# Four graph-network layers on 16 graphs: the first graph's PSUM copies get a chain of their own, and both halves of x are asked for first

## The chip, the core and the metric

The kernel runs on one core of one Trainium2 chip. The metric is the device time of one launch in microseconds. Times inside the profile count from the start of the profiled execution's span. The engines are called by the profile's names: PE (TensorE, matmuls and transposes), DVE (VectorE), ACT (ScalarE), POOL (GpSimd, which here mostly issues gathers), SP (SyncE, which issues most DMAs).

## The reference

There are 16 graphs with 1024 nodes and 64 features each: x is [16, 1024, 64], adj is [16, 1024, 1024] with weights between 0.05 and 1 on about 0.8% of its places and on the diagonal; all is float32. Four layers follow each other, each on the layer norm of what is there so far, and each is added to it:

```python
h = max(layernorm(x), 0); x = x + (adj @ h) @ W.T                  # layer 0
h = max(layernorm(x), 0)                                           # layer 1
m = relu(relu(h @ W1 + b1) @ W2 + b2); msg = relu(adj @ m)
x = x + gru(msg, h)                    # sigmoid gates r and z, tanh n
h = max(layernorm(x), 0)                                           # layer 2
T2 = 2 * adj @ (adj @ h) - h
x = x + (K0*h + K1*(adj @ h) + K2*T2) @ weight + bias
h = max(layernorm(x), 0)                                           # layer 3
# neighbours of a node: adj > 0 off the diagonal; a node with m > 10 of them
# drops every ceil(m/2)-th (and is dropped from theirs)
agg = 0.25*quantile25 + 0.5*quantile50 + 0.25*quantile75           # over neighbours, per feature
x = x + relu((h + agg) @ W1 + b1) @ W2 + b2
```

## The kernel before, in words

**A planner orders the work.** The kernel is written as Python generators, called chains. Each yields one instruction at a time, or a wish for a buffer from a stock, or a condition that it waits for, or a new key. The class `Weave` takes the heads of all chains, works out when each could start by costs that are written into the code (`Line.cost`: a DMA costs 0.4 us to issue, and its data count as there 2.0 us + bytes/150e3 later), picks the engine whose head can start first, and of its heads the one with the smallest key. The order in which instructions are picked is the order in which the engine runs them: every engine works its list from first to last. `Weave.ready` finds when an instruction can start from what earlier ones read and wrote. It compares ranges from the first to the last element, so two interleaved halves of a tile count as one place. The hardware's own waits come from the real places; the planner's view only sets the order. Nearly all instructions of the profile carry line 325, the line of the helper that emits them, so they are told apart by their tiles.

**The chains.** `transposing` loads the adjacency of a graph in eight blocks of 128 columns (512 KB each, on SP) and transposes them: per block two halves, of four PE transposes into one PSUM bank each (stock "tp" with two banks), then an ACT copy of the bank into the tile AT (L952), after which the bank goes back to its stock. The first eight blocks of the run are asked for at once: two in the tiles "block", six in tiles "G". `layering` runs `layers` for two graphs in turn: x is loaded into X in two halves, to even and odd places of the tile (L995–996), normalized (for graph 0 in a form that runs on DVE but for one ACT square root, `sd`), and multiplied with the AT tiles (`into`, one pair of matmuls for each tile; the aggregate goes from its bank to "wide"). Layers 1 and 2 follow. `coding` and `listing` turn AT into lists of neighbours (`there`, `code`, `cand`, `more`, `own`); the list `own` of a graph is done when DVE has converted it to integers. `gathering` then issues 72 indirect DMAs on POOL for each graph (L665) that fetch the neighbours' rows from the table which the graph's layer 2 has stored (L671). `quantiling` sorts them on DVE, and the closing layers and the store of out follow. At the end come a few gathers and scatters for nodes with many neighbours. A general path for other inputs stands under a condition and isn't run.

**Around the change.** Before the chains begin, weights are loaded and prepared: among others the DVE instructions for `k02ident` (L572) and four copies at L587 out of PSUM banks that the transposes need afterwards. In SP's list the first half of x stands first, then two blocks and five of the G blocks, then the second half of x, then the sixth G block. In ACT's list the square root `sd` of graph 0 stands between the third and the fourth copy into AT. The planner counts the second half of x as waiting for the first, as both write to the same range by its reckoning.

Of the kernel before, what the change touches and what calls it, by code (L numbers as in the profile page):

```python
# [16 lines left out]
AF = mybir.ActivationFunctionType  # L17
# [5 lines left out]
P = 128  # L23
N = 1024
NT = N // P
# [116 lines left out]
def batcher(n):  # L142

    full = 1
    while full < n:
        full *= 2
    layers, p = [], 1
    while p < full:
        k = p
        while k >= 1:  # L150
            layer = [(i + j, i + j + k) for j in range(k % p, full - k, 2 * k) for i in range(k)
                     if (i + j) // (2 * p) == (i + j + k) // (2 * p) and i + j + k < n]
            if layer:
                layers.append(layer)
            k //= 2
        p *= 2
    return layers


def needed(layers, places):  # L160

    live, kept = set(places), []
    for layer in reversed(layers):
        k = [(a, b, a in live, b in live) for a, b in layer if a in live or b in live]
        for a, b, _, _ in k:
            live |= {a, b}
        kept.append(k)
    return kept[::-1]


def progressions(s):

    found, top = [], max(s) + 1
    for st in sorted(s):
        found.append((frozenset([st]), (st, 0, 1, 0, 1)))
        for d in range(1, top):
            run = [st]
            while run[-1] + d in s:
                run.append(run[-1] + d)
                found.append((frozenset(run), (st, 0, 1, d, len(run))))  # L180
                for e in range(d * (len(run) - 1) + 1, top):
                    both, k = list(run), 1
                    while all(x + k * e in s for x in run):
                        both += [x + k * e for x in run]
                        k += 1
                        found.append((frozenset(both), (st, e, k, d, len(run))))
    return found
# [164 lines left out]
class Weave:  # L352
# [19 lines left out]
    def add(self, gen, key):  # L372
        self.chains.append(dict(gen=gen, key=key, op=None, want=None, value=None))
# [82 lines left out]
    def run(self):  # L456
        while True:
            before = None
            while before != (before := [(id(c["want"]), id(c["op"])) for c in self.chains]):
                for chain in sorted(self.chains, key=lambda c: c["key"]):  # L460
                    if not self.advance(chain):
                        self.chains.remove(chain)
            heads = [c for c in self.chains if c["op"]]
            if not heads:
                break
            best = {}
            for c in heads:
                op = c["op"]
                c["start"] = max(self.free.get(op.line, 0.0), op.ready)
                best[op.line] = min(best.get(op.line, 1e9), c["start"])  # L470
            line = min(best, key=best.get)
            chain = min((c for c in heads if c["op"].line is line and c["start"] <= best[line] + SLACK),
                        key=lambda c: c["key"])
            op, start = chain["op"], chain["start"]
            chain["op"], chain["value"] = None, self.issue(op, start, (chain["gen"].__name__, chain["key"]))
        assert not self.chains, [c["want"] for c in self.chains]
# [15 lines left out]
class Fast:  # L492
# [431 lines left out]
    def transposing(self, adj):  # L924

        D, T, S = self.D, self.T, self.S
        blocks = {}


        early = self.early  # L930

        def load(i):
            b, j = divmod(i, NT)
            blocks[i] = block = early.pop(0).rearrange("p (t m) -> p t m", m=P) if 2 <= i < NT else (yield "block")
            yield D.dma_start(block, adj[b, :, j * P:(j + 1) * P].rearrange("(t p) m -> p t m", p=P))

        total = GRAPHS * NT
        yield -1.0
        for i in range(NT):
            yield from load(i)  # L940
        for i in range(total):
            b, j = divmod(i, NT)
            yield float(b) - 3
            if NT <= i + 1 < total:
                yield from load(i + 1)
            block = blocks.pop(i)
            at = yield "AT"
            for half in range(2):
                bank = yield "tp"
                for q in range(4):  # L950
                    yield T.transpose(bank[:, q * P:(q + 1) * P], block[:, 4 * half + q, :], self.ident)
                yield S.activation(at[:, 512 * half:512 * half + 512], bank, AF.Copy)  # L952
                self.weave.give("tp", bank)
            if not 2 <= i < NT:
                self.weave.give("block", block)
            self.turned[b].append(at)

    def norm(self, w, h, X, then=None, early=False, order=range(NT)):

# [28 lines left out]
    def layers(self, w, b, x):  # L988

        T, V, S, D, give = self.T, self.V, self.S, self.D, self.weave.give  # L990
        ident = self.ident
        cols = [slice(0, 512), slice(512, N)]
        yield lambda: self.turns == b
        X = yield "X"
        for half in range(2):  # L995
            yield D.dma_start(X[:, half::2, :], x[b, cols[half], :].rearrange("(q p) f -> p q f", p=P))
        turned = self.turned[b]
        by_tile = [2 * (j % 4) + j // 4 for j in range(NT)]

# [26 lines left out]
        bank = yield "fm"  # L1026
# [6 lines left out]
        bank = yield "fm"  # L1033
# [8 lines left out]
        bank = yield "fm"  # L1042
# [8 lines left out]
        bank = yield "fm"  # L1051
# [4 lines left out]
        bank = yield "fm"  # L1056
# [37 lines left out]
        for v in (new, z):  # L1094
            first, bank = bank if sides else None, (yield "fm")
# [16 lines left out]
        bank = yield "fm"  # L1112
# [4 lines left out]
        bank = yield "fm"  # L1117
# [34 lines left out]
        bank = yield "fm"  # L1152
# [7 lines left out]
        X = last  # L1160
# [291 lines left out]
    def run(self, x, adj, nodemask, out):  # L1452
        self.out = out
        self.listed, self.paid, self.gathered, self.last, self.turns = {}, {}, [], [], 0
        self.fetched = []
        self.masked, self.coded = [0] * GRAPHS, {}
        self.turned = [[] for _ in range(GRAPHS)]
        self.sizes = dict.fromkeys(("hits", "bad", "m1", "pos", "off", "coef"), 0)
        for t, n in CLASSES + MANY:
            places = max(int(np.ceil(tau * (n - 1))) for tau in TAUS) + 1  # L1460
            for name, size in (("hits", 2 * (n - 1) * t), ("bad", (n - 1) * t), ("m1", t), ("pos", 4 * t),
                               ("off", 4 * places * t), ("coef", places * t)):
                self.sizes[name] = max(self.sizes[name], size)
        add = self.weave.add
        add(self.listing(nodemask), 0.0)
        add(self.transposing(adj), 0.0)
        add(self.coding(), 0.0)
        for w in range(2):
            add(self.layering(w, x), 0.0)
        add(self.gathering(), 0.0)  # L1470
        add(self.fetching(), 0.0)
        add(self.quantiling(), 0.0)
        self.weave.run()
# [624 lines left out]
```

## Time and profile before

| what | value |
|---|---|
| time, median of three runs | 1920.10 us (1913.11, 1920.10, 1929.66) |
| profiled execution | 1915.65 us, its span 1913.6 us |
| mean granted PE clock | 0.836 |
| DVE busy | 1616.6 us, 84% |
| PE busy | 1418.7 us, 74% |
| POOL busy | 1357.5 us, 71% |
| ACT busy | 1015.5 us, 53% |
| first transposes on PE, first gather on POOL | at 13.03 us, at 125.83 us |

A line of the timeline gives start and duration in us, the engine, the line, the operation, the tile written and the tiles read, how many alike follow each other, and in brackets for how long the engine stood idle before it and what ended that. A line of the list of waits gives the engine, its tile and line, what it waited for, then the sum, the number of times and the longest, in us. A line of the chain of waits gives start and duration in us of a piece of the path that ended last.

### The profile page before, as it was taken

How to read it: one execution, taken by the hardware profiler on the slowest of the kernel's cores; microseconds unless marked ns; L12 is line 12 of the kernel's file. 1: busy time of each engine (PE TensorE's matmuls, PEld its weight loads, DVE VectorE, ACT ScalarE, POOL GpSimd, SP SyncE). 2: the span in 40 equal slices, each digit the busy share in tenths (PEclk: the TensorE clock that was granted, in tenths of full speed). 3: DMA queues.
4: the chain of work that ended last, by engine and by line, in shares of the span. 5: the costliest groups of instructions: out<-in, count | busy, mean ns of one | idle time of the engine just before them, and what ended most of it. 6: DMA issues, size and time to landing. Idle time of an engine off the chain costs nothing.

```text
span 1913.6 us, 24539 instructions
## 1 busy us (share of the span) xinstructions
PE 1418.7 (74%) x6740; PEld 742.3 (39%) x6740; DVE 1616.6 (84%) x4699; ACT 1015.5 (53%) x2905; POOL 1357.5 (71%) x1315
## 2 busy tenths in 40 slices
PE   6888688878887988888888888888787853442314
PEld 2343335343434453434444444444343422231313
DVE  2755998769899889898999999998999899898866
ACT  3656666575766566666666575666666431121000
POOL 2027777777777777777777777777777777777772
PEclk8989797989998889899989898989999786556555
DMA  5233525343535444434444443435252413121110
GB/s 140 77 78 81 95 70 95 80 79 74 112 86 74 90 72 103 72 93 82 94 73 102 68 106 64 100 68 96 67 108 46 56 24 44 36 40 39 26 27 12
DMA packets 260192, 141.10 MB, mean 74 GB/s; under 512 B 91370, under 2 KB 239328, under 8 KB 260048
## 3 DMA queue, kind: packets, MB, share of 16 engines
q1 hardware_dynamic: 216720, 94.40, 21.2%
q0 software_dynamic: 42064, 44.37, 15.0%
q8 instruction: 57, 0.93, 0.2%
q10 hardware_dynamic: 1264, 0.68, 0.1%
q14 instruction: 87, 0.71, 0.1%
HBM read 120.18 MB, written 19.17 MB: 73 GB/s over the span
## 4 chain that ended last, share of the span: by engine, by line
DVE 57%; PE 19%; ACT 8%; issue 6%; DMA 5%; POOL 4%; SPq 0%; DVEq 0%; POOLq 0%; ACTq 0%
DVE G L325 22%; PE bank L325 19%; DVE net L325 7%; DVE L L325 4%; DVE cand L325 4%; ACT sq L325 4%; DVE wide L325 4%; POOL G L665 4%; DMA G<-table,own 3%; DVE st L325 2%; DMA X<-in_x 2%; DVE AT L325 1%; ACT there L325 1%; ACT L325 1%; DVE off L325 1%
## 5 line engine op out<-in xcount | busy, mean ns | idle before, releaser
L665 POOL DMA_INDIRECT G<-table,own x1274 | 1327.5, 1042 | 516.9 <-issue 299.9
L325 PE MATMUL bank<-AT,nodes 128*64 128x512 f32 x2048 | 576.9, 638 | 38.5 <-ACT nodes L325 30.3
L325 PE MATMUL bank<-G,c 128*128 128x256 f32 (+2 forms) x646 | 183.0, 423 | 148.1 <-DVE G L325 148.1
L325 PEld LDWEIGHTS bank<-AT,nodes 128*64 128x64 f32 x2048 | 162.9, 144 | 290.3 <-issue 190.5
L325 PE MATMUL bank<-c,block 128*128 128x128 f32 x976 | 194.3, 307 | 56.4 <-ACT AT L325 45.9
L325 DVE TENSOR_TENSOR G<-G 128x256 f32<-128x256 f32 (+5 forms) x401 | 211.2, 546 | 7.7
L325 PEld LDWEIGHTS bank<-c,block 128*128 128x128 f32 x976 | 128.3, 154 | 207.4 <-issue 138.8
L325 PEld LDWEIGHTS bank<-G,c 128*128 128x128 f32 x646 | 123.9, 233 | 192.8 <-DVE G L325 125.5
L325 ACT ACTIVATE AT<-bank 128x512 f32<-128x512 f32 x256 | 150.3, 588 | 84.8 <-PE bank L325 84.1
L325 ACT ACTIVATE nodes<-X,off,ri 128x64 f32<-128x64 f32 x360 | 140.9, 430 | 67.2 <-DVE off L325 67.2
L325 ACT ACTIVATE G<-G,coef 128x64 f32<-128x64 f32 x384 | 97.8, 339 | 108.8 <-DVE coef L325 108.8
L325 ACT ACTIVATE sq<-X,st 128x64 f32<-128x64 f32 x360 | 125.0, 347 | 48.3 <-DVE st L325 27.3
L325 DVE TENSOR_TENSOR net<-G 128x512 f32<-128x512 f32 (+8 forms) x246 | 143.5, 601 | 4.3 <-PE bank L325 1.4
L325 DVE TENSOR_TENSOR G<-G,net 128x512 f32<-128x512 f32 (+4 forms) x235 | 136.0, 598 | 4.6
L325 PE MATMUL bank<-wide,blocks 128*128 128x512 f32 x224 | 124.4, 656 | 20.0 <-DVE wide L325 11.8
L325 ACT ACTIVATE there<-AT 128x1024 f16<-128x1024 f32 x128 | 133.4, 1050 | 0.4
L325 PE MATMUL bank<-there,c 128*64 128x512 f16 x256 | 76.7, 431 | 59.3 <-DVE there L325 55.5
L325 ACT ACTIVATE off<-off 128x144 f32<-128x144 f32 (+5 forms) x76 | 22.9, 301 | 152.4 <-DVE off L325 151.2
L325 DVE SCALAR_TENSOR_TENSOR G<-bad,G 128x512 f32<-128x512 f32 (+2 forms) x161 | 100.4, 684 | 0.0
L325 DVE MAX8 L<-cand 128x8 f16<-128x103 f16 x384 | 91.8, 263 | 8.7
L325 ACT ACTIVATE wide<-bank 128x512 f32<-128x512 f32 (+2 forms) x86 | 49.0, 570 | 89.7 <-PE bank L325 89.5
L325 PE MATMUL bank<-wide,yo 64*64 64x128 f32 x512 | 64.7, 383 | 34.8 <-DVE wide L325 33.2
(216 smaller groups left out, 2226.1 us busy)
## 6 DMA issues: line engine op xcount, KB each, us to landing
block<-in_adj SPq DMA_DIRECT2D x122, 512.0 KB
G<-table,own POOLq DMA_INDIRECT x1274
rows<-pay SPq DMA_DIRECT2D x16, 632.0 KB
table<-pay SPq DMA_DIRECT2D x16, 264.0 KB
X<-in_x SPq DMA_DIRECT2D x32, 128.0 KB
yo<-rows SPq DMA_DIRECT2D x16, 256.0 KB
out<-yo SPq DMA_DIRECT2D x16, 256.0 KB
G<-in_adj SPq DMA_DIRECT2D x6, 512.0 KB
```

The lines of the kernel that those rows point to most:

```text
L325: return Op(self, lambda: f(*args, **kwargs), writes, reads, cost, later)
L665: return self.nc.gpsimd.indirect_dma_start(out=out, out_offset=None, in_=table, in_offset=bass.IndirectOffsetOnAxis(ap=at, axis=0))
```

## The change

There are two edits. In `transposing`, the copies of graph 0's banks into AT are no longer yielded behind the transposes: half, tile and bank are noted in `self.raw`, and a new chain, `copying`, yields the copies, gives the banks back and hands the finished tiles over. The tiles of later graphs are copied as before, but are handed over only when all eight tiles of graph 0 have been. In `layers`, the second half of x is told to the planner as writing nothing. So the planner lets it be issued without waiting for the first, and doesn't count the time until its data are there; that is so for all 16 graphs. Real dependencies are kept.

```diff
@@ transposing @@
                 for q in range(4):
                     yield T.transpose(bank[:, q * P:(q + 1) * P], block[:, 4 * half + q, :], self.ident)
+                if b == 0:
+                    self.raw.append((half, at, bank))
+                    continue
                 yield S.activation(at[:, 512 * half:512 * half + 512], bank, AF.Copy)
                 self.weave.give("tp", bank)
             if not 2 <= i < NT:
                 self.weave.give("block", block)
-            self.turned[b].append(at)
+            if b:
+                yield lambda: len(self.turned[0]) == NT
+                self.turned[b].append(at)
+
+    def copying(self):
+        yield -3.0
+        for i in range(2 * NT):
+            yield lambda: len(self.raw) > i
+            half, at, bank = self.raw[i]
+            yield self.S.activation(at[:, 512 * half:512 * half + 512], bank, AF.Copy)
+            self.weave.give("tp", bank)
+            if half:
+                self.turned[0].append(at)
@@ layers @@
         for half in range(2):
-            yield D.dma_start(X[:, half::2, :], x[b, cols[half], :].rearrange("(q p) f -> p q f", p=P))
+            load = D.dma_start(X[:, half::2, :], x[b, cols[half], :].rearrange("(q p) f -> p q f", p=P))
+            if half:
+                load.writes = []
+            yield load
@@ run @@
-        self.fetched = []
+        self.fetched, self.raw = [], []
...
         add(self.transposing(adj), 0.0)
+        add(self.copying(), 0.0)
```

Comparing the lists of both kernels: POOL's is the same throughout. In SP's list both halves of x of graph 0 now stand first, ahead of the blocks. In ACT's list `sd` stands ahead of all sixteen copies, and one table load is gone. In PE's list sixteen transposes come first, then pairs of matmuls alternate with eight transposes, and ten matmuls stand together at the end, where before a pair followed each set of four transposes. In DVE's list the seven instructions of graph 0's normalization stand among the preparations, the last of them ahead of `k02ident` and L587, and the first sum over X of a later graph stands earlier in three places. All lists are the same again from about the fifth graph on.

## The prediction

> **What bounds the kernel now.** I read the page first, to see which engines are full; then the table of stretches and the timeline of the first 50 us, since the diff edits only the first graph's work there; then the chain of waits over the first 130 us, to learn whether that start is on the path; and last the list of waits, to learn whether a shift of the start can reach the end.
>
> The page:
>
> ```profile
> span 1913.6 us, 24539 instructions
> PE 1418.7 (74%) x6740; PEld 742.3 (39%) x6740; DVE 1616.6 (84%) x4699; ACT 1015.5 (53%) x2905; POOL 1357.5 (71%) x1315
> DVE 57%; PE 19%; ACT 8%; issue 6%; DMA 5%; POOL 4%; SPq 0%; DVEq 0%; POOLq 0%; ACTq 0%
> ```
>
> The vector engine is the fullest and holds 57% of the chain that ended last. The list of waits says what POOL, the engine of the gathers, waits for:
>
> ```profile
> POOL G L665 <- issue: 299.9, 984, 0.3
> POOL G L665 <- DVE own L325: 110.7, 1, 110.7
> POOL G L665 <- PE bank L325: 47.2, 116, 2.3
> DVE st L325 <- DMA X<-in_x: 28.0, 11, 6.3
> ```
>
> POOL is idle for 110.7 us once, until the first gather at 125.83, and never again for more than 2.3 us: from there gathers follow each other every 0.95 + 0.30 = 1.25 us up to about 1881. So a first gather that comes earlier can move everything behind it, as long as each graph's table is ready when POOL gets to it.
>
> The start, in the timeline:
>
> ```profile
> 12.30 2.39 SPq L325 DMA_DIRECT2D X<-in_x  x1
> 16.73 1.28 ACT L325 ACT_TABLE_LOAD   x1
> 19.71 0.69 DVE L325 TENSOR_REDUCE st<-X 128x8 f32<-128x512 f32 x1 [6.05 <-DMA X<-in_x]
> 23.59 0.30 ACT L325 ACTIVATE sd<-va,eps 128x8 f32<-128x8 f32 x1 [5.59 <-DVE va L325]
> 24.43 1.11 PE L325 MATMUL bank<-c,G 128*128 128x128 f32 x4 [7.02 <-ACT AT L325]
> 30.08 0.66 PE L325 MATMUL bank<-c,G 128*128 128x128 f32 x4
> 43.38 2.80 PE L325 MATMUL bank<-AT,nodes 128*64 128x512 f32 x12
> 47.63 0.57 ACT L325 ACTIVATE wide<-bank 128x512 f32<-128x512 f32 x1
> ```
>
> The second half of x is asked for at 12.30, behind blocks that fill SP's queue. Its sum starts at 19.71; the normalization reaches the scalar engine (sd) at 23.59. That engine's order puts sd between copies of transposed tiles, so they stand still too, both transpose banks stay full, and TensorE idles 7.02 us. The chain of waits confirms it: the path runs through this X, then through 19 us of TensorE.
>
> ```profile
> 12.30 7.32 DMA X<-in_x
> 24.43 19.03 PE bank L325 x64
> ```
>
> **The change, part by part.** Comparing the issue orders of both kernels, engine by engine, the same instructions are there, except one table load fewer on the scalar engine. POOL's order is the same throughout; VectorE's is the same for the last 3226 entries of its list of 4442, TensorE's for the last 3267 of 4785, SyncE's from its 74th of 225. The differences end in about graph 5, near 550 us. Nothing later waits for a fixed time, so the end moves by what is left of the shift there.
>
> (1) X first. SP issues both halves at about 0.75 and 1.25 (the first half is asked for at 0.75 now). Landing: no row shows the second half so early. The late one took 7.32 with a full queue, which gives 8.6 as the upper bound; the first weight that TensorE waited for, asked for at 1.24, was there at 6.17, which I take. VectorE's chain (0.69 + 0.15 + 0.67 + 0.67 + 0.67 + 0.20 + 0.69 = 3.74 us, from its rows) then stands ahead of the constant k02ident and the four copies of L587 (1.36), which free the PSUM that the transposes wait for. They began at 13.03; I take 14.0 (13.0 if X is there at 5, 16.0 if at 8.6).
>
> What is late: the eight blocks, by 128 KB at the 266 GB/s of the stretch 0–25 us = 0.5 us. The last is needed by TensorE near 28 and lands near 22. Cover gone, the cost is 0.5.
>
> The Trainium skill, "DMA: Bandwidth & Descriptors", speaks against small rows ahead of larger ones: by Specifications a transfer below 512 B doesn't reach line rate, and "Why small descriptors are slow (HBM only)" gives a 256 B descriptor 27% overhead. A row of X is 64 floats, 256 B; by the rule the 0.5 us would be an estimated 0.6, and hidden as well. No run here shows the two rates apart.
>
> (2) Copies apart. Sixteen copies of 0.60 us follow each other now without sd in between, and TensorE's order changes: the first sixteen transposes of a tile pair still take 3.57, one pair of aggregation matmuls 0.93; then five rounds of eight transposes and a pair (1.32 + 0.93) plus eight more transposes, 12.6; then ten matmuls at 0.43 plus 0.2 of tail, 4.5. That is 21.6 us, from 14.0 to 35.6. Before, it ended at 43.38 + 2.80 = 46.2. Gain 10.6; with the starts of 13.0 and 16.0, 11.6 and 8.6. Of the gain 7.0 is the stall; 0.9 is the two slow sets of transposes after it (1.11 and 1.12 against 0.66); the rest is closer packing. The table load saved (1.28) costs nothing now: it lies in the wait for sd.
>
> (3) To the first gather. The aggregate's copy moves from 47.63 to about 37. Behind it, the scalar engine works without gaps worth naming until 63.50 (code), VectorE is 88% busy from 75 to 100 and TensorE 86% there and 91% from 100 to 125; block loads for graph 1 are triggered by transposes that are early too. So the whole 10.6 should reach 125.83. The new wait on graph 0's tiles costs nothing: they are all copied before graph 1's first tile is.
>
> (4) Given back. The scheduler no longer counts the landing of the second half, so it believes that a later graph's X is ready sooner. On VectorE, which is in order, three of the sums over a new X now stand right behind the conversion of own, the running graph's neighbours; queued behind that sum are the rest of the previous layer's add and of the running list of neighbours. The rows of before at the three places, and what follows the first:
>
> ```profile
> 131.31 0.69 DVE L325 TENSOR_REDUCE st<-X 128x8 f32<-128x512 f32 x1 [6.31 <-DMA X<-in_x]
> 181.21 0.24 DVE L325 TENSOR_TENSOR hits<-G,own 128x80 f32<-128x80 f32 x1 [8.18 <-DMA G<-table,own]
> 308.09 0.20 DVE L325 CAST own<-own 128x80 int32<-128x80 f32 x1
> 314.00 0.68 DVE L325 TENSOR_REDUCE st<-X 128x8 f32<-128x512 f32 x1
> 409.81 0.69 DVE L325 TENSOR_REDUCE st<-X 128x8 f32<-128x512 f32 x1 [4.59 <-DMA X<-in_x]
> ```
>
> At 131 four instructions (some 2 us), and at most 3.5 us with the smaller ones around them, move behind a wait that stays as long; they go into the 8.18 us that VectorE waits at 181.21. At 314.00 there is no wait now; moved up behind the conversion at 308.09, the sum waits up to 314.0 − 308.3 = 5.7. That is 0 to 5.7; I take 0, because from 325 to 425 VectorE is idle for 31 us (busy 69.18 of 100) and POOL needs the next table only 16 us after it is ready (399.34 against 415.52). At 409.81 the conversion stands at 399.34 and the sum would be reached at 400.4, so its wait grows from 4.6 to 9.4, by 0 to 4.8; afterwards VectorE is over 90% busy and a loss stays. I take the middle, 2.4, since POOL's margin of 14 to 16 us there covers a part.
>
> **Sum:** −10.6 + 2.4 = −8.2 us on the profiled execution, 1915.65 (span 1913.6 and 2.05 around it): 1907.4. The runs' median, 1920.1, is 4.5 above this execution; the same shift on it gives 1911.9, rounded 1912. Bounds: −11.6 + 0 and −8.6 + 5.7 + 4.8, so −12 to +2, or 1908 to 1922.
>
> **The rivals.**
>
> *A, hidden.* A start that is early ends in a wait for another engine. For: from graph 7 on the table is ready only 0.7 to 2.6 us before POOL needs it (802.91 against 805.76), so both sides bind, and a lag on either eats the gain. Against: both sides start early here. Price: the whole 8; 1918 to 1922, that is, about 1920.
>
> *B, more than the start.* POOL's 47.2 us of waits for TensorE's banks shrink because graphs 1 to 4 interleave better. If a fifth goes, −10.6 − 9.4 = −20: 1900. Against: each of these waits is small and most lie where the orders are alike.
>
> *C, slower.* The three sums of step 4 hold up VectorE's queue and nothing takes it in: 3.5 + 5.7 + 4.8 = 14.0 us lost, against a start gain of 8.6 to 10.6. That is +3.4 to +5.4, 1924 to 1926. It decides from the point where the conversion of own in graph 5 (600.93) comes later than before. For: VectorE holds 57% of the chain. Against: the wait at 181 and the idle time from 325 to 425.
>
> *D, not what it says.* Later graphs' halves are issued back to back already (398–400), so only graph 0's request moves. But the wait of 7 us is graph 0's, so this takes nothing away.
>
> **How the numbers follow.** My forecast, a gain of 4 to 12: 0.58. A: 0.15. B: 0.13. C: 0.14. Some 1% (19 us) is about what a measurement of this kernel can tell from no change; its three runs lie within 1913.11 and 1929.66. Faster than 1901: a fifth of the forecast's cases, by such scatter, 60% of B's and few of A's: 0.21. Slower than 1939: a third of C, by scatter: 0.05. The rest is 0.74. The range takes in the bounds 1908 to 1922, B's 1900 and most of C; the likeliest case's own range is 1908 to 1916.
>
> **What would show it.** Right: the first st<-X near 6 to 9 us, no TensorE gap above 2 us between 14 and 36, the first gather between 113 and 118, then the first gather of graph 5 (610.14) 6 to 12 earlier. Step 4 is seen in the wait of st<-X: it sums to 28.0 now, 7.1 of it before 30 us; above 21 + 14 = 35 C is at work. The prediction is wrong if the first gather moves by less than 6, or if it moves by 10 and the last gather doesn't.

## The result, and the profile after

The changed kernel is slower: a median of 1930.77 us over 20 runs (1912.48 to 1947.51) against 1916.51 us (1902.32 to 1939.40) over 20 runs of the kernel before on the same chip. The ratio is 1.0078, with a 95% interval of 1.0050 to 1.0107: some 15 us lost. This ratio, like those below, leaves out runs that took over 1.5% more than the fastest of their kernel, so it can differ from the quotient of the medians beside it, most for `x_first_again` below, where 5 of 12 runs are left. Its profiled execution took 1943.40 us, 12.6 above its own median, while that of before stood within 1 us of its median; so of the difference of the two profiles, 28 us, nearly half is the scatter of single executions.

The page of the kernel after:

```profile
span 1941.6 us, 24545 instructions
PE 1455.9 (75%) x6740; PEld 771.1 (40%) x6740; DVE 1615.1 (83%) x4699; ACT 1016.9 (52%) x2904; POOL 1358.7 (70%) x1315
DVE 51%; PE 23%; ACT 8%; DMA 6%; issue 6%; POOL 5%; SPq 1%; DVEq 0%; POOLq 0%; ACTq 0%
```

DVE, POOL and ACT are busy for as long as before. PE is busy for 37 us more with the same 6740 matmuls, and its share of the chain that ended last rose from 19% to 23%. The mean granted clock of PE is 0.814, where it was 0.836. So the same matmuls took longer. The list of waits:

```profile
POOL G L665 <- issue: 298.4, 978, 0.6
POOL G L665 <- PE bank L325: 174.2, 124, 97.0
DVE st L325 <- DMA X<-in_x: 37.9, 12, 11.0
```

The one long wait of POOL, until its first gather, is 97.0 us now (it was 110.7). The profile puts it down to a PE bank instead of `own`, so it stands in the second line; without it that line is 77.2, against 47.2 before. The timeline of the start, and the first gather:

```profile
0.75 0.99 SPq L325 DMA_DIRECT2D X<-in_x  x2
4.96 0.69 DVE L325 TENSOR_REDUCE st<-X 128x8 f32<-128x512 f32 x1 [1.98 <-DMA X<-in_x]
7.88 1.28 ACT L325 ACT_TABLE_LOAD   x1 [7.88 <-DMA wide<-in_L_gnn_W_hh]
9.85 0.30 ACT L325 ACTIVATE sd<-va,eps 128x8 f32<-128x8 f32 x1 [0.69 <-DVE va L325]
13.53 3.62 PE L325 MATMUL bank<-c,block 128*128 128x128 f32 x16 [1.13 <-issue]
29.24 4.51 PE L325 MATMUL bank<-AT,nodes 128*64 128x512 f32 x20
111.82 1.01 POOL L665 DMA_INDIRECT G<-table,own  x1 [96.98 <-PE bank L325]
```

The start did what it was to do. X is there at 4.96, `sd` runs before the first copy, the aggregation ends at 29.24 + 4.51 = 33.75 instead of 46.2, and the first gather comes at 111.82 instead of 125.83: 14.0 us won. Then they are lost. A good clock for that are the sixteen stores of the table at L671, one for each graph, in the timeline of SP:

| issue of the table's store, us | before | after | difference |
|---|---|---|---|
| graph 0 | 120.4 | 106.7 | −13.7 |
| graph 3 | 397.7 | 383.4 | −14.3 |
| graph 5 | 595.3 | 593.3 | −2.1 |
| graph 9 | 992.3 | 996.0 | +3.7 |
| graph 12 | 1287.7 | 1306.9 | +19.2 |
| graph 15 | 1580.1 | 1608.1 | +28.0 |

From the last store to the end of the span both take 333.5 us. So 12 us went between graphs 3 and 5, where the orders of the two kernels still differ, and 30 between graphs 5 and 15, where all lists are the same. The three places that the prediction's step 4 named, in the timeline of the kernel after, with the two gaps of PE that go with the second and third:

```profile
115.69 0.69 DVE L325 TENSOR_REDUCE st<-X 128x8 f32<-128x512 f32 x1 [5.82 <-DMA X<-in_x]
167.59 0.24 DVE L325 TENSOR_TENSOR hits<-G,own 128x80 f32<-128x80 f32 x1 [4.42 <-DMA G<-table,own]
302.09 0.69 DVE L325 TENSOR_REDUCE st<-X 128x8 f32<-128x512 f32 x1 [2.84 <-DMA X<-in_x]
303.95 0.68 PE L325 MATMUL bank<-wide,yo 64*64 64x128 f32 x2 [10.29 <-DVE wide L325]
393.35 0.69 DVE L325 TENSOR_REDUCE st<-X 128x8 f32<-128x512 f32 x1 [5.13 <-DMA X<-in_x]
401.95 0.64 PE L325 MATMUL bank<-there,c 128*64 128x512 f16 x2 [7.62 <-DVE there L325]
```

The wait of 8.18 at 181.21 has become 4.42 at 167.59: it took in the first place, as argued. At 302.09 there is a new wait of 2.84; PE, which needs a `wide` that is queued behind it on DVE, stands still for 10.29 us there, and for 4.07 at this place in the kernel before. At 393.35 the wait grew only from 4.59 to 5.13, and PE's 7.62 us behind it stand against 10.08 before.

What a wait of DVE for X does to PE can be read where it stands alone. The timeline of the kernel after at graph 10, from SP's, DVE's and PE's lines:

```profile
1094.05 0.37 SPq L671 DMA_DIRECT2D table<-pay  x1
1094.50 0.54 SPq L671 DMA_DIRECT2D rows<-pay  x1
1095.10 2.73 SPq L325 DMA_DIRECT2D X<-in_x  x2
1107.64 0.69 DVE L325 TENSOR_REDUCE st<-X 128x8 f32<-128x512 f32 x1 [3.42 <-DMA X<-in_x]
1109.16 0.64 PE L325 MATMUL bank<-there,c 128*64 128x512 f16 x2 [4.80 <-DVE there L325]
1110.53 3.67 PE L325 MATMUL bank<-wide,yo 64*64 64x128 f32 x30 [0.73 <-DVE wide L325]
1131.21 7.98 PE L325 MATMUL bank<-AT,nodes 128*64 128x512 f32 x32
```

X is asked for right behind 264 KB of table and 632 KB of rows on the same queue and is there 12 us later. DVE waits 3.42 us for it, PE 4.80 for DVE. And from then on PE is slow. The table of stretches of the kernel after; the last two columns are DMA, the one before them is the granted clock:

```profile
1100.00:1110.00 10.00, 5.00 (x30) 3.73 (x29) 5.89 (x26) 8.09 (x30) 7.30 (x8) 0.96 0.95 119
1110.00:1120.00 10.00, 9.47 (x46) 6.42 (x47) 9.18 (x45) 5.21 (x13) 5.37 (x6) 0.50 0.28 74
1120.00:1130.00 10.00, 10.00 (x30) 6.14 (x30) 3.97 (x20) 4.54 (x11) 3.82 (x5) 0.50 0.45 93
1140.00:1150.00 10.00, 9.60 (x38) 4.27 (x37) 9.87 (x26) 6.50 (x11) 7.56 (x9) 1.00 0.30 76
```

and the same instructions in the kernel before, one graph earlier, where PE had waited 0.82 us for `there`:

```profile
1010.00:1020.00 10.00, 9.92 (x53) 6.00 (x55) 9.07 (x48) 7.91 (x20) 7.56 (x8) 1.00 0.64 160
1020.00:1030.00 10.00, 8.35 (x40) 2.96 (x37) 9.34 (x36) 5.31 (x20) 7.68 (x8) 1.00 0.26 53
```

After the gap the clock is 0.50 and stays there for over 20 us, until the long run of matmuls on AT at 1131, although PE is busy the whole time. DVE (3.97 of 10) and POOL (3.82 of 10) now wait for PE. It isn't an artifact of the clock's records: two matmuls `bank<-wide,blocks` took 2.08 us there, and 1.12 in the kernel before. Such a stretch stood in five of the kernel after's intervals between table stores from graph 4 to graph 13, which took 105.7 to 108.6 us, and in one of the kernel before (103.4); from graph 3 on the intervals of both kernels without one took 96 to 101. That is some 5 to 12 us for each stretch. In the last interval, from graph 14 to 15, both kernels have one and it cost nothing that shows (97.7 and 97.8 us). The kernel after has seven half-clock stretches of 15 us or more between 100 and 1600 us, the kernel before four.

The Trainium skill, "TensorE: Matmul & The Clock Gate", section "What's actually happening", has the clock fall after at least one idle window of about 3.4 us and return after about 3.4 us of sustained work. The first half agrees with the 4.80 us here, but two of the other stretches (from 1215.0 and 1320.8 us) began behind gaps of 2.48 and 2.33 us. The second half doesn't agree: 20 us of busy PE at 0.50 are measured.

### The profile page after: what moved, and what is told of

Its sections match the earlier page's. It is cut to its first block, busy times and chain, and to the rows that moved or that the text cites. A ratio compares the mean times of both kernels' runs of the same rounds, so it can differ in the third digit from the quotient of the medians.

```text
span 1941.6 us, 24545 instructions
## 1 busy us (share of the span) xinstructions
PE 1455.9 (75%) x6740; PEld 771.1 (40%) x6740; DVE 1615.1 (83%) x4699; ACT 1016.9 (52%) x2904; POOL 1358.7 (70%) x1315
## 4 chain that ended last, share of the span: by engine, by line
DVE 51%; PE 23%; ACT 8%; DMA 6%; issue 6%; POOL 5%; SPq 1%; DVEq 0%; POOLq 0%; ACTq 0%
PE bank L325 23%; DVE G L325 20%; DVE net L325 6%; POOL G L665 4%; DVE wide L325 4%; ACT sq L325 4%; DVE cand L325 3%; DVE L L325 3%; DMA G<-table,own 2%; DMA X<-in_x 2%; DVE st L325 2%; DVE AT L325 1%; ACT there L325 1%; DVE off L325 1%; DVE there L325 1%
## 5 line engine op out<-in xcount | busy, mean ns | idle before, releaser
L325 PE MATMUL bank<-AT,nodes 128*64 128x512 f32 x2048 | 590.1, 651 | 38.0 <-ACT nodes L325 30.4
L325 PEld LDWEIGHTS bank<-AT,nodes 128*64 128x64 f32 x2048 | 172.1, 147 | 289.5 <-issue 185.6
L325 PE MATMUL bank<-wide,yo 64*64 64x128 f32 x512 | 69.3, 393 | 29.3 <-DVE wide L325 27.9
```

Source lines behind the costliest of these rows:

```text
L325: return Op(self, lambda: f(*args, **kwargs), writes, reads, cost, later)
```

## The experiments

They came in five groups; each ratio is to runs of the kernel before in the same group. In the first, fourth and fifth group every kernel, the one before too, had a median of 2116 to 2141 us. The list of waits of the unchanged kernel after shows in the fourth group what is at most 1.2 us in the other two: PE waiting a hundred times for its own instructions.

```profile
PE bank L325 <- issue: 105.3, 99, 4.4
```

Why some groups ran so isn't known; the first, third and fourth group ran on one chip, so it isn't the chip alone. They are read apart from the others.

### First group (before: 2125.07 us): the start alone, and the loads' order

`x_first` keeps the order of before, except that SP issues the second half of graph 0's x right behind the first (`both` makes two DMAs at one place of SP's list). `after_late` is the kernel after with a start that is too long. `after_x_chain` and `before_x_chain` load x in a chain of its own, which the planner knows of, so that it reorders.

```diff
 x_first (against before)
+        if b == 0:
...
+            def both():
+                made.append(first())
+                made.append(second())
...
+            loads[0].make, loads[1].make, loads[1].early = both, lambda: made[1], True
 after_late (against after)
-            nc.vector.memset(blocks, 0.0)
+            for _ in range(14):
+                nc.vector.memset(blocks, 0.0)
 after_x_chain, before_x_chain
+    def loading(self, x):
+        yield -4.0
+        for b in range(GRAPHS):
+            X = yield "X"
...
+            self.fresh[b] = X
```

> The kernel before, with one thing changed: the second half of graph 0's x is issued right behind the first. Every later instruction on every engine keeps the order of before. The start should gain 7.0 us of idle TensorE and 0.9 us of slow transposes, less 0.5: about 7.4 us at the first gather. Theory 1 (a shift of the start is kept to the end): the whole time falls by 6 to 8 us, ratio 0.996 to 0.997. Theory 2 (what costs is the order of graphs 2 to 5, which is that of before here): the same, 0.996. Theory 3 (the time is set by how many graphs run their layers at TensorE's half clock after the wait for X; each such stretch of 20 us or more costs 7 to 10 us, and where the windows of the clock fall is chance): between 0.99 and 1.01, and the time of the profiled run follows its number of such stretches, not the 7.4 us.

> The changed kernel with 13 more fills of a constant tile on VectorE ahead of everything, about 14.6 us, so that its first gather comes at about 124 to 125, as in the kernel before; all orders are those of the changed kernel. Theory 1: slower than the changed kernel by 12 to 15 us, some 1945, ratio 1.014. Theory 2: the same. Theory 3: between the changed kernel's 1.008 and 1.016 by its number of stretches at half clock.

> The changed kernel, with the loads of X in a chain of their own: the X of a later graph is asked for as soon as its tile is free, ahead of the stores of table and rows on the sync engine's queue, not behind them. VectorE's waits for X near the conversion of own should go (eleven of 1 to 6 us), and with them TensorE's idle time ahead of the products of `there`. Theory 3: fewer long stretches at half clock, 10 to 25 us less than the changed kernel, ratio 0.995 to 1.003 against the kernel before. Theory 2: graph 5's 10 us come back, ratio near 1.003. Theory 1: only the waits for X themselves, 3 to 5 us, ratio 1.005.

> The kernel before with the same chain for the loads of X and nothing else. Theory 3: VectorE's waits for X go and long stretches at half clock become fewer; 5 to 15 us faster than before, ratio 0.992 to 0.997. Theories 1 and 2: as before but for the waits for X of graphs 2 and 5 (11 us of waits, part of them hidden), ratio 0.996 to 1.000.

| kernel | first gather, us | median, us | ratio (95%) |
|---|---|---|---|
| x_first | 117.16 | 2115.79 | 0.9960 (0.9944–0.9976) |
| after_late | 128.38 | 2133.82 | 1.0052 (1.0032–1.0072) |
| after_x_chain | 108.76 | 2124.80 | 0.9999 (0.9977–1.0021) |
| before_x_chain | 125.58 | 2121.55 | 0.9987 (0.9969–1.0006) |

With the order of before, an earlier start is kept: the first gather is 125.83 − 117.16 = 8.7 us earlier than in the profile of before, and 0.4% of 2125 is 8.5 (5 to 12 by the interval). With the order of after it isn't: `after_late` starts 2.6 us late and ends 0.5%, 11 us, late. So about 8 us are lost behind the start, in the order. The ratios expected of `after_late` and `after_x_chain` were built on the 1.008 of the kernel after; a group in which PE waits for its instructions doesn't show that loss, and both came out below them. The two chains of loads change the order in more places; `after_x_chain` has the earliest first gather of all and gains nothing. They show no more than that the start doesn't decide.

### Second group (before: 1943.59 us): is it PE's clock?

`after_again` and `x_first_again` are the kernels of above. `before_warm` and `after_warm` put twelve matmuls with zeros into the gap of PE ahead of the first matmul on `there` of each graph but the first; they add zero to its bank and cost the planner nothing, so the order stays.

```diff
+                fill = 12 if j == 0 and b > 0 else 0
+                for i in range(fill):
+                    op = T.matmul(bank[0:NB, :], self.zero16, self.ones16, start=i == 0, stop=False)
+                    op.cost, op.later, op.reads, op.writes = 0.0, 0.0, [], []
+                    yield op
...
```

> The changed kernel itself, to stand beside the others on one chip. Theory 1 (a shift of the start is kept to the end): where x_first gained 0.4% for 8.4 us at its first gather, this one, 14 us early, gains 0.6% but for 2 to 5 us of waits: ratio 0.994 to 0.998. Theory 2 (the order in graphs 2 to 5 costs some 20 us more than the start gains): slower, 1.005 to 1.010. Theory 3 (the number of long stretches at TensorE's half clock sets it): slower where it has more such stretches than the kernel before, equal or faster where both have one in nearly every graph.

> The kernel before with the second half of graph 0's x issued right behind the first, and all later orders as before. Theories 1 and 2: 7 to 9 us faster than before, ratio 0.995 to 0.997. Theory 3: the same where every graph has its long stretch at half clock anyway; where only some have one, between 0.99 and 1.01.

> The kernel before, with 12 products of a zero tile (adding nothing to the sums) put on TensorE ahead of the first product of `there` in each of graphs 1 to 15, where TensorE stands idle for 1 to 6 us and its clock falls; the orders of everything else are those of before. Cost: 12 x 0.21 us, 2.6 us a graph where nothing is idle, at most 38 us in all. Theory 3: the clock doesn't fall there; each long stretch at half clock that goes brings 7 to 12 us: ratio 0.98 to 0.995 where few graphs have one, 0.92 to 0.97 where nearly all have. Theories 1 and 2: nothing gained, 1.000 to 1.015.

> The changed kernel with the same 12 products of a zero tile. Theory 3: the stretches go, and with them what the change lost: 0.975 to 0.99 of the kernel before, and below before_warm by the start's 10 us (0.5%). Theory 2: above before_warm by 0.8%. Theory 1: equal to the changed kernel or slower.

| kernel | median, us | ratio (95%) | DVE's waits for X, us |
|---|---|---|---|
| after_again | 1950.67 | 1.0060 (1.0005–1.0116) | 53.9 |
| x_first_again | 1936.25 | 0.9895 (0.9837–0.9952) | 42.6 |
| before_warm | 1922.62 | 0.9917 (0.9874–0.9961) | 28.9 |
| after_warm | 1934.59 | 0.9970 (0.9927–1.0012) | 58.5 |

The loss came again, if barely clear of 1, and `x_first` is faster again (0.9962 by the medians of all runs), so it isn't the start. The filling made both kernels 0.8 to 0.9% faster (1.0060 to 0.9970, and 1 to 0.9917): the clock costs both of them time. In the profile of `before_warm` no half-clock stretch of 15 us or more is left between 100 and 1480 us; in that of `after_warm` there are four, from 210, 521, 1118 and 1323 us. But it left the difference between the two orders, 0.5%, as it was. So the gap ahead of `there` isn't the whole of it. The timeline of `after_again`, at the second and third of step 4's places, has longer waits than the first profile:

```profile
312.18 0.69 DVE L325 TENSOR_REDUCE st<-X 128x8 f32<-128x512 f32 x1 [6.50 <-DMA X<-in_x]
314.03 0.69 PE L325 MATMUL bank<-wide,yo 64*64 64x128 f32 x2 [13.96 <-DVE wide L325]
405.05 0.69 DVE L325 TENSOR_REDUCE st<-X 128x8 f32<-128x512 f32 x1 [6.65 <-DMA X<-in_x]
413.57 0.64 PE L325 MATMUL bank<-there,c 128*64 128x512 f16 x2 [9.07 <-DVE there L325]
```

And in graph 5 the profiles of the two orders part. First the PE lines of the kernel after:

```profile
501.16 0.41 PE L325 MATMUL bank<-there,c 128*64 128x512 f16 x2 [3.00 <-DVE there L325]
502.04 1.97 PE L325 MATMUL bank<-wide,yo 64*64 64x128 f32 x16 [0.47 <-DVE wide L325]
504.45 1.97 PE L325 MATMUL bank<-wide,yo 64*64 64x128 f32 x14 [0.43 <-ACT yo L325]
...
523.42 8.09 PE L325 MATMUL bank<-AT,nodes 128*64 128x512 f32 x32
```

then those of `x_first_again`, which has the order of before:

```profile
505.02 0.64 PE L325 MATMUL bank<-there,c 128*64 128x512 f16 x2 [7.32 <-DVE there L325]
506.74 1.97 PE L325 MATMUL bank<-wide,yo 64*64 64x128 f32 x16 [1.07 <-DVE wide L325]
508.64 1.11 PE L325 MATMUL bank<-c,block 128*128 128x128 f32 x4
...
512.40 0.66 PE L325 MATMUL bank<-c,block 128*128 128x128 f32 x4
...
520.05 3.65 PE L325 MATMUL bank<-AT,nodes 128*64 128x512 f32 x16
```

Here four transposes take 1.11 us at 508.64 and 0.66 at 512.40: the clock is back within 8 us of the gap's end at 505.02, in spite of the longer gap. In the new order PE stops once more between the two runs on `yo`, and the clock is 0.50 until the run on AT, over 20 us later. The interval between the table stores of graphs 4 and 5 shows it: 108.6, 111.0 and 109.9 us in the kernel after, `after_again` and `after_warm`, against 98.9, 103.1 and 101.2 in the kernel before, `x_first_again` and `before_warm`.

### Third group (before: 1936.80 us): X ahead of the stores

`after_quiet` and `first_quiet` (the latter on `x_first`) let SP ask for the x of graphs 2 to 15 just ahead of the table and rows that another graph stores. The planner isn't told, so no other engine's order changes. `after_burst` puts eight matmuls with zeros ahead of the run on `yo` instead. `first_quiet_burst` does both on `x_first`.

```diff
 after_quiet, first_quiet
+            if b >= 2:
+                load.make, load.early = (lambda half=half: self.asked[b][half]), True
...
-        yield self.store(b, "table", table, pay[:, :, H:H + R])
+        store = self.store(b, "table", table, pay[:, :, H:H + R])
+        if b + 2 < GRAPHS:
+            put = store.make
+            def ask():
...
+                for half in range(2):
+                    ins = self.nc.sync.dma_start(own_x[:, half::2, :], x[b + 2, cols[half], :]...)
...
+                ins = put()
...
+                return ins
+            store.make = ask
+        yield store
 after_burst
+                for i in range(8 if k == 0 else 0):
+                    op = T.matmul(bank[0:NB, :], self.zero16, self.ones16, start=True, stop=True)
...
```

> The changed kernel; on the sync engine's queue the X of graphs 2 to 15 is asked for ahead of the stores of table and rows, not behind them. The planner isn't told, so the order of all other engines is that of the changed kernel. VectorE's waits for X (13 of them, some 40 us in the last profile of the changed kernel) should go. Theory 2 (the loss is made in graphs 2 to 5, where VectorE stands in line for X): the early waits go and with them some 10 us up to the fifth table, ratio 0.995 to 1.000 against the kernel before. Theory 3 (what counts is the half clock after TensorE's idle time ahead of `there`): that idle time shrinks and fewer long stretches follow, ratio 0.985 to 0.995. If the waits for X aren't the cause: 1.004 to 1.010, as the changed kernel.

> The kernel before with the second half of graph 0's x first, and X of graphs 2 to 15 ahead of the stores; all else in the order of before. Theories 2 and 3: the start's 8 us and a part of the waits for X: ratio 0.980 to 0.992 (x_first alone had 0.9895 and 0.996). If the waits for X cost nothing: as x_first.

> The changed kernel with 8 products of a zero tile (adding nothing to the sums) right ahead of the 32 products of yo in each graph, so that TensorE's run without a break after the idle time is 7 us long at half clock, not 3.6. Theory 3, in the form that the clock comes back only after a run without a break that covers a window of some 3.4 us: no stretch at half clock of 8 us or more in graphs 6 to 14, graph 5's included (103 us from its table to the next, not 109 to 111); 0.99 to 1.00 against the kernel before, 8 us less for each stretch that goes and 1.7 to 3.4 us more for each graph. If the length of the run isn't what decides: stretches as before, and slower than the changed kernel by up to 40 us, 1.01 to 1.03.

> All three together on the order of before: the second half of graph 0's x first, X ahead of the stores, the 8 products ahead of yo. If theories 2 and 3 both hold, the fastest of the kernels: 0.975 to 0.990. If the fill costs more than the stretches that are left: slower than first_quiet by 5 to 20 us.

| kernel | median, us (range) | ratio (95%) | DVE's waits for X, us |
|---|---|---|---|
| after_quiet | 1890.27 (1884.50–1894.14) | 0.9833 (0.9768–0.9898) | 12.6 |
| first_quiet | 1888.23 (1887.52–1890.11) | 0.9823 (0.9763–0.9884) | 8.6 |
| after_burst | 1918.99 | 0.9959 (0.9915–1.0004) | 53.4 |
| first_quiet_burst | 1891.95 | 0.9840 (0.9778–0.9901) | 9.4 |

`first_quiet` is the fastest version of all and beats both kernels by 1.8% and more. The page's line of DMA issues (KB each, and the median time from issue to landing in us) of the kernel after, and then of `after_quiet`:

```profile
X<-in_x SPq DMA_DIRECT2D x32, 128.0 KB, 8.8
```

```profile
X<-in_x SPq DMA_DIRECT2D x32, 128.0 KB, 2.5
```

Ahead of the stores X is there in 2.5 us instead of 8.8. The Trainium skill, "DMA: Bandwidth & Descriptors", section "Queues, rings and completion order", says that each DMA engine takes the descriptors of one issuing queue in the order of its ring; the two medians agree with that.

One edit that touches nothing but the moment of these requests moves the new order from 1.006–1.008 to 0.983, some 45 us, and the order of before with the early start from 0.9895 to 0.9823, some 14 (each ratio has its 0.6% to either side, and the medians of all runs give 0.996 to 0.975, some 40, for the latter). It also takes the scatter away: `after_quiet`'s 6 runs spread over 10 us, the 18 of before in the same group over 59. So the waits for X cause most of the loss and of the scatter. That they cost the new order more rests on a comparison across groups, and how much more isn't settled. What is left between the two orders, with no waits for X behind the start, is small: 0.1%, and `after_quiet`'s first gather is 3.4 us earlier (112.06, 115.41), together about 5 us. Graph 5 alone has more: `after_quiet`'s interval is still 107.9 us with no wait for X, and `first_quiet`'s is 99.0. `after_burst` brings this interval down to 102.4, has no half-clock stretch of 8 us or more from 425 to 1520 us, as one of its expected cases had it, and its ratio is 1 to 1.2% below that of the new order alone. Its waits for X are as long as ever, and its median is 29 us above that of `after_quiet`; the zeros cost little where that was measured (`first_quiet_burst` is 3.7 us above `first_quiet`). That points to a price of the waits beside that of the clock.

### Fourth and fifth group (before: 2140.68 and 2126.87 us): where do the waits for X cost?

`after_quiet_2to5` and `after_quiet_6on` ask early for the x of graphs 2 to 5, or from 6 on. `before_quiet` does it for all, without the early start; `after_third` is the kernel after. The fifth group ran two of them again.

```diff
 after_quiet_2to5
+            if 2 <= b <= 5:
...
 after_quiet_6on
+            if b >= 6:
...
```

> The changed kernel with X asked for ahead of the stores for graphs 2 to 5 only, the graphs whose order the change moved; from graph 6 on as in the changed kernel. If what the change lost is made in these graphs' waits for X: 8 to 16 us less than the changed kernel, ratio 0.996 to 1.001 against the kernel before. If it is made later, by the waits for X and the half clock of graphs 6 to 15: as the changed kernel, 1.004 to 1.010.

> The other half: X ahead of the stores for graphs 6 to 15 only. If the loss is made in graphs 2 to 5: what the later waits and stretches cost in either kernel comes back (20 to 35 us), the early loss stays: 0.988 to 0.997. If the later graphs alone made it: 0.983, as with all graphs.

> The kernel before with X of graphs 2 to 15 ahead of the stores and the start as it was. It prices the start with little scatter left: first_quiet (0.9823) came 0.4 to 0.5% below this if the 8 us at the first gather are kept to the end, so 0.986 to 0.988 here; 0.982 if they are lost.

> The changed kernel on the same chip: 1.004 to 1.010, as in the two measurements of it so far.

> The changed kernel with X ahead of the stores for graphs 2 to 5 only, once more, since TensorE in the last measurement waited 100 us and more for its instructions, which hid the waits for X. Where it doesn't: 0.996 to 1.001 against the kernel before if the loss is made in graphs 2 to 5, 1.004 to 1.010 if it is made later. Where it does again: 0.995, as last time.

> The kernel before with X of graphs 2 to 15 ahead of the stores, once more: 0.986 to 0.988 if the waits for X and the clock bind and the start's 8 us are kept (first_quiet had 0.9823); near 1.000 where TensorE waits for its instructions, as last time.

| kernel | median, us | ratio (95%) |
|---|---|---|
| after_quiet_2to5 | 2129.83 | 0.9951 (0.9931–0.9971) |
| after_quiet_6on | 2135.06 | 0.9975 (0.9958–0.9991) |
| before_quiet | 2140.35 | 1.0003 (0.9987–1.0020) |
| after_third | 2133.78 | 0.9972 (0.9955–0.9990) |
| after_quiet_2to5_b | 2117.42 | 0.9950 (0.9930–0.9969) |
| before_quiet_b | 2127.66 | 0.9995 (0.9977–1.0012) |

These groups missed what they were for, since PE waited for its instructions again, and the intervals from graph 3 on had medians of 112 to 114 us whatever X did. They show the other side: where PE is held up anyway, asking early for X is worth nothing to the kernel before (1.0003 and 0.9995) and little to the kernel after, DVE waits less for X (23.7 us in `after_third`), and the change is faster, by 0.3%, 6 us of its 13 at the start (first gather 112.48). How the loss divides between graphs 2–5 and the later ones was not measured where it occurs.

## Why the prediction was wrong, point by point

**Steps 1 to 3, the start: right, and a little too small.** Transposes began at 13.53 (14.0 forecast), the stream took 20.2 us (21.6) and ended 12.4 us earlier (10.6), and the first gather came 14.0 us earlier. X was there sooner (its sum began at 4.96; 6 to 9 was named), which gives 0.5 of the 1.8 us more; the shorter stream gives the rest. `x_first` shows that such a gain is carried to the end when the order stays. One reading was a little off: POOL's later waits in the kernel before reach 2.55 us (at 1196.97), not 2.3.

**Step 4, what is given back: this is the step that failed.** It was 2.4 us with bounds 0 and 10.5. From table store to table store, graphs 0 to 5, it measured:

| kernel | order of before, us | order of after, us |
|---|---|---|
| as it is | 474.9 (before) | 486.6 (after) |
| again | 480.4 (x_first_again) | 500.9 (after_again) |
| gap ahead of `there` filled | 480.6 (before_warm) | 500.0 (after_warm) |
| X asked for early | 467.0 (first_quiet) | 474.6 (after_quiet) |

So 12 to 20 us are given back there by the first three rows, in place of 2.4, and the start is used up by graph 5's table. Two terms were mis-sized.

The place at 308 was put at nothing, because DVE has idle time around it. It measured a wait of 2.84 and 6.50 us, and the gap of PE behind it, 4.07 in the kernel before, grew to 10.29 and 13.96 (7.36 in `after_quiet`, so 3.3 of the growth is the order, and the rest, 2.9 and 6.6, goes with the wait). The wait reaches the next table's store: from graph 2's to graph 3's took 87.8 us in `after_quiet`, which has no such wait, 90.8 in the kernel after and 94.6 in `after_again`, 3.0 and 6.7 more. So DVE's idle time was no cover, since PE waits for what is queued behind the sum. The differences between the two orders hide this, since without the wait the new order is the faster one in this interval (87.8, against 94.8 in `first_quiet` and 95.1 in the kernel before).

And no price was set at all on a slower PE. The step costed waits in DVE's time alone, with every matmul at its duration from the profile of before; but the same matmuls take nearly twice as long for 20 us after some of these gaps. In graph 5, from its predecessor's table to its own, the new order takes 8 to 10 us more in all four rows. There it is the new order itself, without a wait for X, that keeps the clock low (107.9 against 99.0 with X asked for early), and with zeros ahead of `yo` it takes 102.4. The place at 409.81, put at 2.4, had its wait grow by 0.5 and 2.1.

**"Nothing later waits for a fixed time, so the end moves by what is left of the shift": wrong.** Transfers of X wait behind the stores in every graph, and a graph's time isn't fixed: it is some 98 us or some 105, as the clock either returns within 8 us or stays low for 20, and which of the two changes from run to run of one kernel (from graph 10 to 11, 107.0 us in the kernel after and 96.4 in `after_again`). The pair of profiles loses 30 us between graphs 5 and 15 with equal lists. How much of that is the change's isn't settled: `x_first_again`, with the order of before, took 1007.6 us for these ten graphs, `after_again` 999.3, the kernels before and after 984.7 and 1014.9. The medians ask for about 15 + 14 − 17 = 12 us here (17 is the mean of the table's first three differences). With X asked for early it is 973.4 in `first_quiet` and 964.6 in `after_quiet`. At the gathers the loss shows one graph later than at the stores: the first gather of graph 5 still came 9.9 us earlier (600.26), inside the 6 to 12 that were named as a sign of being right, that of graph 6 only 2.3, and the last gather came 27.5 us later (1904.57 against 1877.11). That is the prediction's own sign of being wrong: the first gather moved by 14 and the last didn't follow.

**The rivals.** C had the right place, the three sums over X in DVE's list, and named a loss. Its sign for the waits, above 35 us, is passed by 37.9 only by luck: 13.0 of it stand before 30 us, 10.98 of that in one wait at 26.84 behind the start. What is left, 24.9, is to be held against 21 in the kernel before and the named 35. In `after_again` it is 40.9 of 53.9, and the sign is passed. But its price, 14.0 us, was in DVE's time again, and its point of decision didn't hold: the conversion of `own` in graph 5 comes at 598.91, still earlier than 600.93, and the kernel is slower all the same. B's place, POOL's waits for PE's banks, moved the other way, from 47.2 to 77.2 us. A doesn't hold: the start arrived at the first gather, and in `x_first` such a gain is kept to the end. D takes nothing away, as it said itself.

**Left open.** What decides whether the clock returns within 8 us or after 20 isn't shown. The broken run on `yo` goes with the long stretches in graph 5 in all four profiles of the new order that have no zeros ahead of that run and no waits of PE for its instructions, but a run in one piece (3.67 us at 1110.53) didn't prevent one in graph 10. The kind of the matmuls is a rival to the length of the run: in `after_burst` the clock was back 3.2 us after a gap of 5.04 in graph 5, during 3.3 us of zeros with 128x64 weights and 512 columns. Nor were the two edits of the change tried one without the other, so which of them makes the new order slow isn't shown; that it is the half that the planner no longer waits for is step 4's reading.

## What to carry to other kernels

Where a planner is told that a load is there earlier than it is, the consumer moves ahead in an in-order engine's list; follow that list to the next instruction that another engine needs, and price the wait as that engine's idle time, and as a slower TensorE behind it. A small load that is needed soon belongs ahead of the large stores of its queue: together with the early start that was worth 1.7 to 1.8% here, where the start alone measured 0.4% and 1.0%, and it made the runs alike. Where PE was held up by its own instructions it was worth nothing to the kernel before. When a kernel's runs scatter by 2% and the mean granted clock goes along with it (here 0.833 to 0.813 over the 20 runs of the kernel after, the lowest in the longest), look for TensorE's gaps before trusting a change of a few microseconds.

## What was not expected of the hardware

- PE stayed at a clock of 0.50 for 20 to 24 us while it was 95 to 100% busy with small matmuls, after gaps of 2.33 to 4.80 us; for the same instructions it also came back within 8 us after a gap of 7.32.
- The constant `k02ident` took 0.39 us on DVE at 11.03, and 1.96 at 9.55 in the kernel before, where a memset of POOL (9.54 to 11.42) ran beside it. That the memset is the cause isn't shown: in the kernel after a sum (0.68 us at 9.14) and a product (0.69 at 10.42) ran beside the same memset at their usual time.
- In three of the five groups PE waited about 100 times for its instructions, 105 us in all in the unchanged kernel after, and the kernels that ran in both kinds of group took 9 to 12% longer there.
